# The linear term of three integration stages moved from TensorE to ScalarE and GpSimd, and one clamp from VectorE to GpSimd

## The chip, the cores and the metric

The kernel runs on one core of a Trainium2 chip. The metric is the device time of one execution in microseconds. A core has TensorE (PE, with weight loads listed apart as PEld), VectorE (DVE), ScalarE (ACT), GpSimd (POOL) and SyncE (SP), which issues the DMAs. Each engine works through its own queue in order, and semaphores tie the queues together.

## What is computed

Two layers, each a token mixer followed by a feed-forward block. The change lies in the mixer of the first layer, a coupled oscillator integrated over 32 time steps with the classical fourth-order Runge-Kutta rule. The state is q and p, of 128 batch rows by 256 features; x gives the drive of each step.

```python
def _derivative(q, p, drive, coupling, bias):
    i_couple = jnp.tanh(q) @ coupling.T
    dq = q - q ** 3 / 3.0 - p + drive + i_couple + bias
    dp = EPSILON * (q + ALPHA - BETA * p)
    return (dq, dp)

def _rk4_step(q, p, drive, coupling, bias):
    dq1, dp1 = _derivative(q, p, drive, coupling, bias)
    dq2, dp2 = _derivative(q + 0.5 * DT * dq1, p + 0.5 * DT * dp1, drive, coupling, bias)
    ...
    q_next = q + DT / 6.0 * (dq1 + 2 * dq2 + 2 * dq3 + dq4)
    p_next = p + DT / 6.0 * (dp1 + 2 * dp2 + 2 * dp3 + dp4)
    q_next = jnp.clip(q_next, -CLAMP, CLAMP)
    p_next = jnp.clip(p_next, -CLAMP, CLAMP)
    return (q_next, p_next)
```

Every q of the 32 steps then goes through a feed-forward block with block-quantized operands, and is added to x. The second layer (attention within a row's 32 tokens, then a feed-forward block with Hadamard rotations) follows on all 4096 tokens.

## The kernel before

The kernel has two phases. The first takes the 32 steps one after the other: `step` integrates q and p, and `ffn0` does the feed-forward block of that step's q and prepares the normalized, transposed input of the second layer (`xnT`). `ffn0` feeds nothing back into the recurrence, so it may run behind it, as far as its buffers reach. The second phase takes the 4096 tokens in 32 groups; its first item waits for the last `xnT`. Early in the first phase the weights of the first layer are quantized (POOL and DVE), from about step 24 on those of the second (ACT and DVE).

Nothing is issued in the order in which it is written. Every operation is an item with an engine, a cost in microseconds, the buffers that it reads and writes, and a rank. `Work.order` plans all items of both phases: a list scheduler, run forwards and backwards 40 times with priorities from the run before, that keeps the order with the earliest modelled end. Buffers take slots from pools (`slim`: 18 of 128x256 in SBUF; `ps_sum`: 3 of 128x256 in PSUM; `ps_stage`: 2 banks; `states`: 6), so a pool also limits how far work can run ahead. Where the plan leaves PE idle, small matmuls on zeros (L1354) are put in.

A step has four slopes. Slope i takes a state q_i (q, q2, q3, m4) and makes

- tanh of q_i on ACT (L594), and from it four 128x128 matmuls with the coupling matrix (L601, eight records each time since the data is fp32), which add to the PSUM tile `ps[i]`;
- a scaled square of q_i on ACT (L595), and from it the cube, square times q_i, on POOL (L608).

The next state is a `nest` (L552, one DVE operation: first operand times a constant, plus or minus the second) of `ps[i]` and the cube; after the fourth slope the new q is made by a saturating sum on DVE (L645). Into `ps[i]` go further an opening matmul on zeros (L497), a nest with p, x or w for the old state, and `plus` (L587): a matmul of a scaled identity with the drive or with a state. The eye matmuls `plus(1, 1, q2)`, `plus(2, 2, q3)` and `plus(3, 5, m4)` carry the linear term that belongs to the slope at q2, q3 and m4. `plus(3, 4, q3)` and the four with the drive are others. The slope at q has no such matmul: its linear term is in the constants K.

p is carried scaled and shifted. x, w and z are sums in PSUM that later stages need; z, which becomes the next p, is built in place over p by four nests, and is clamped in place on DVE (L653) at the end of the step. The next step's first nests read p and the new q.

Per step, `ffn0` adds on PE a transpose of q, eight bf16 512-column matmuls (L929), eight 256-column ones (L976) and a transpose; on DVE block maxima, scalings and clips; on POOL the multiplications by block scales (L914, L956, L964), the root (L993, L994) and, but for the last five steps, gain and shift (L1003, L1007).

Of the kernel before, what the change touches and what calls it, by code (L numbers as in the profile page):

```python
# [14 lines left out]
AF = mybir.ActivationFunctionType  # L15
ALU = mybir.AluOpType
# [4 lines left out]
P = 128  # L21
# [5 lines left out]
CLAMP = 20.0  # L27
# [12 lines left out]
PE, DVE, ACT, POOL, SP = "PE", "DVE", "ACT", "POOL", "SP"  # L40


def rk4():

    h, m = DT, DT * EPSILON  # L50

    def unit(i):
        return [float(i == n) for n in range(5)]

    def lin(*terms):
        return [sum(a * v[n] for a, v in terms) for n in range(5)]

    P1, q, Q2, Q3, Q4 = (unit(i) for i in range(5))
    s1 = lin((1.0, q), (-BETA, P1))
    P2 = lin((1.0, P1), (m / 2.0, s1))  # L60
    s2 = lin((1.0, Q2), (-BETA, P2))
    P3 = lin((1.0, P1), (m / 2.0, s2))
    s3 = lin((1.0, Q3), (-BETA, P3))
    P4 = lin((1.0, P1), (m, s3))
    s4 = lin((1.0, Q4), (-BETA, P4))
    end = lin((1.0, P1), (m / 6.0, s1), (m / 3.0, s2), (m / 3.0, s3), (m / 6.0, s4))
    last = lin((-1 / 3, q), (1 / 3, Q2), (2 / 3, Q3), (1 / 3, Q4), (-h / 6.0, P4))
    return P2, P3, end, last
# [31 lines left out]
class Work:  # L100
# [17 lines left out]
    def add(  # L118
        self, engine, cost, fn, reads=(), writes=(), fills=(), rank=0.0, table=None, port=False,
        tail=0.0, after=(), records=8, small=False, behind=(),  # L120
    ):
        item = Item(engine, cost, fn, rank, table, port, tail, records)
        item.small, item.behind = small, behind
        needs = list(after)
        for b in reads:
            needs += b.writers
        for b in writes:
            needs += b.writers + b.readers
        for b in reads:
            b.readers.append(item)  # L130
        for b in (*writes, *fills):
            b.writers.append(item)
        item.bufs = list(dict.fromkeys((*reads, *writes, *fills)))
        item.outs = (*writes, *fills)
        for b in item.bufs:
            b.left += 1
        item.after = list(dict.fromkeys(needs))
        self.items.append(item)
        return item
# [183 lines left out]
def kernel(  # L323
# [22 lines left out]
    nc = tc.nc  # L346
# [13 lines left out]
    def tile_of(name, shape, dtype=F32):  # L360
        return const.tile(shape, dtype, name=name)


    def slots(name, n, count, dtype=F32):
        return [Slot(tile_of(f"{name}{i}", [P, n], dtype)) for i in range(count)]
# [8 lines left out]
    slim = slots("slim", N, 18)  # L374
# [8 lines left out]
    def banks(name, n, count):  # L383

        tiles = [ps_1.tile([P, HALF], F32, name=f"{name}{i}") for i in range(-(-count * n // HALF))]
        return [
            Slot(t[:, k : k + n], f"{name}{i}") for i, t in enumerate(tiles) for k in range(0, HALF, n)
        ][:count]
# [3 lines left out]
    ps_sum = banks("ps_sum", N, 4)  # L392
# [29 lines left out]
    add = work.add  # L422
# [15 lines left out]
    def two(ap):  # L438
        return ap.rearrange("p (c k) -> p c k", c=NC)
# [38 lines left out]
    P2, P3, END, LAST = rk4()  # L478
    S = -END[4]
    h = DT  # L480
    K = (1.0 + h / 2, 1.0 - h / 2 * P2[1], 1.0 - h * P3[1])
    EYES = (h / 2 / K[0], h / 2 / K[1], h / K[2], h / 6, LAST[3], -LAST[4] - h / 6)
    C_SCALES = (*EYES[:3], -h / 6)
    CUBES = tuple((c / 3.0) ** 0.5 for c in (h / 2, h / 2, h, h / 6))
    eyes = []
    for i, c_eye in enumerate(EYES):
        eye = tile_of(f"eye{i}", [P, P])
# [6 lines left out]
    def opened(dst, rank, after=()):  # L494
        add(
            PE, 0.11,
            lambda: nc.tensor.matmul(dst.ap, lhsT=zeros[:, :P], rhs=zeros, start=True, stop=False),  # L497
            [], [dst], rank=rank, after=after,
        )
# [31 lines left out]
    for m in range(NC):  # L531
# [4 lines left out]
        sl = slice(m * P, (m + 1) * P)  # L536
        for i, (c_scale, b_c, c_mat) in enumerate(zip(C_SCALES, b_coup, coup)):
            add(
# [7 lines left out]
    stt = nc.vector.scalar_tensor_tensor  # L546
    MULT, ADD, SUB = ALU.mult, ALU.add, ALU.subtract

    def nest(dst, in0, scalar, in1, rank, op1=ADD):

        reads = [b for b in (in0, in1) if b is not dst]
        add(DVE, 0.335, lambda: stt(dst.ap, in0.ap, scalar, in1.ap, MULT, op1), reads, [dst], rank=rank)  # L552
# [26 lines left out]
    def step(t, q, p, d):  # L579
        rank = t - 500.0  # L580
        ps = [Buf(slots_) for slots_ in ps_stage]
        x, w, z = Buf(ps_sum), Buf(ps_sum), p
        q2, q3, m4, w2, qn = Buf(slim), Buf(slim), Buf(slim), Buf(slim), Buf(states)

        def plus(i, eye, src, cost=0.43):
            return add(
                PE, cost, lambda: nc.tensor.matmul(ps[i].ap, lhsT=eyes[eye], rhs=src.ap, start=False, stop=False),  # L587
                [src], [ps[i]], rank=rank,
            )

        def slope(i, qi):

            th, sq = Buf(slim), Buf(slim)
            add(ACT, 0.32, lambda: nc.scalar.activation(th.ap, qi.ap, AF.Tanh), [qi], [th], rank=rank, table="silu")  # L594
            add(ACT, 0.31, lambda: nc.scalar.activation(sq.ap, qi.ap, AF.Square, scale=CUBES[i]), [qi], [sq], rank=rank)  # L595

            def mm():
                for c in range(NC):
                    for m in range(NC):
                        sl = slice(m * P, (m + 1) * P)  # L600
                        nc.tensor.matmul(  # L601
                            ps[i].ap[:, sl], lhsT=coup[i][:, c, sl], rhs=two(th.ap)[:, c, :],
                            start=False, stop=(c == NC - 1 and m == NC - 1),
                        )

            add(PE, 0.9, mm, [th, b_coup[i]], [ps[i]], rank=rank)
            add(
                POOL, 0.685, lambda: nc.gpsimd.tensor_tensor(sq.ap, sq.ap, qi.ap, MULT),  # L608
                [qi], [sq], rank=rank, port=True,
            )  # L610
            return sq

        for i in range(2):
            opened(ps[i], rank)
            nest(ps[i], p, -h / 2 * (1.0, P2[0])[i] * S / K[i], q, rank)
            if not i:
                started.append(work.items[-1])
            plus(i, i, d)
        nest(x, p, -h * P3[0] * S / K[2], q, rank)
        cube = slope(0, q)  # L620
        nest(w, p, LAST[0] * S / LAST[1], q, rank)
        nest(z, p, END[0] * S / END[1], q, rank)
        nest(q2, ps[0], K[0], cube, rank, SUB)
        plus(1, 1, q2)
        cube = slope(1, q2)
        opened(ps[2], rank)
        nest(ps[2], q2, -h * P3[2] / K[2], x, rank)
        plus(2, 2, d)
        nest(w2, w, LAST[1] / LAST[2], q2, rank)
        nest(z, z, END[1] / END[2], q2, rank)  # L630
        nest(q3, ps[1], K[1], cube, rank, SUB)
        plus(2, 2, q3)
        cube = slope(2, q3)
        opened(ps[3], rank)
        add(ACT, 0.27, lambda: nc.scalar.mul(ps[3].ap, w2.ap, LAST[2]), [w2], [ps[3]], rank=rank)
        plus(3, 3, d)
        plus(3, 4, q3)
        nest(z, z, END[2] / END[3], q3, rank)
        nest(m4, ps[2], -K[2], cube, rank)
        plus(3, 5, m4)  # L640
        cube = slope(3, m4)
        nest(z, z, -END[3] / END[4], m4, rank)
        add(
            DVE, 0.335,
            lambda: nc.vector._custom_dve(  # L645
                TENSOR_ADD_SAT, out=qn.ap, in0=ps[3].ap, in1=cube.ap, s0=CLAMP, s1=-CLAMP
            ),
            [ps[3], cube], [qn], rank=rank,
        )
        edge = ALPHA / BETA  # L650
        add(
            DVE, 0.335,
            lambda: nc.vector.tensor_scalar(  # L653
                z.ap, z.ap, (-CLAMP - edge) / S, (CLAMP - edge) / S, ALU.min, ALU.max
            ),
            [], [z], rank=rank,
        )
        return qn, z


    def mx_scales(amax, nb, rank, mul, inv_slots):
# [360 lines left out]
    p = b_p  # L1022
# [9 lines left out]
    for t in range(T):  # L1032
        d = d_next
        if t + 1 < T:
            x_of[t + 1] = load_x(x_step, t + 1, t - 501.0)
            d_next = drive(t + 1, t - 499.9)
        q, p = step(t, q, p, d)
        ffn0(t, q)
# [378 lines left out]
```

## Time and profile before

| | us |
|---|---|
| median of 3 runs | 867.8 |
| lowest, highest | 867.76, 870.64 |
| the profiled execution | 868.0 |
| its span, first to last instruction | 866.2 |
| busy in the span: PE, PEld | 795.1, 598.6 |
| busy in the span: DVE, ACT, POOL | 732.2, 494.0, 615.9 |

A profile is of one execution, and what is added up from its rows stands against that execution's own time. Busy is the time covered by an engine's records; records of neighbouring instructions overlap, on PE most of all, so a covered engine need not be full. The granted PE clock was 0.986 over the span. In group lines the mean duration of one instruction stands after the busy time, and after the second bar the engine's idle time just ahead of these instructions, with what ended it. In timeline lines the first number is the start, the second how long the piece lasts, and the bracket holds the idle time before it and what ended it.

### The profile page before, as it was taken

The numbers are of one execution on the slowest core, as the hardware profiler recorded it, in microseconds if no ns is written. First come the engines' busy times: TensorE is split into PE (matmuls) and PEld (weight loads), VectorE is DVE, ScalarE is ACT, GpSimd is POOL, SyncE is SP. The second block draws the span as 40 slices with busy tenths as digits, with TensorE's granted clock in tenths as the row PEclk, the third lists the DMA queues.
The fourth block names the chain that finished last, engine by engine and source line by source line (L and its number), as shares of the span: only waits on it lengthen the run. The fifth ranks groups of instructions, "written<-read, shape, count | busy, mean of one in ns | idle before, by whom it ended". The sixth has DMA issues, their size and how long they took to land. (4 is left out here: it accounts for less than half of the span.)

```text
span 866.2 us, 26286 instructions
## 1 busy us (share of the span) xinstructions
PE 795.1 (92%) x10506; PEld 598.6 (69%) x10506; DVE 732.2 (85%) x1863; ACT 494.0 (57%) x1009; POOL 615.9 (71%) x955
## 2 busy tenths in 40 slices
PE   7789999999999999997789999999999999899986
PEld 4566778877788788775456667666667676576765
DVE  6889989999989999998677887778878788887694
ACT  3233465655466665754335667666767555776755
POOL 5698898888768888899574776656685676676320
PEclk9999999999999999999799999999999999999999
DMA  7222232313122242435500113221221221221334
GB/s 241 84 38 53 59 82 59 74 49 83 35 65 68 70 134 56 92 67 110 117 2 15 27 39 65 49 49 32 52 50 48 56 48 42 48 43 46 60 68 86
DMA packets 128891, 55.53 MB, mean 64 GB/s; under 512 B 102144, under 2 KB 127616, under 8 KB 128768
## 3 DMA queue, kind: packets, MB, share of 16 engines
q1 hardware_dynamic: 128768, 53.85, 26.9%
q8 instruction: 82, 1.34, 0.6%
q14 instruction: 41, 0.34, 0.1%
HBM read 21.32 MB, written 8.39 MB: 34 GB/s over the span
## 5 line engine op out<-in xcount | busy, mean ns | idle before, releaser
L1294 POOL TENSOR_TENSOR wide<-wide 128x512 f32<-128x512 f32 x116 | 149.1, 1306 | 68.7 <-DVE wide L1278 33.6
L601 PEld LDWEIGHTS ps_stage<-slim,coup 128*128 128x128 f32 x1024 | 129.3, 192 | 18.1 <-ACT slim L594 10.6
L601 PE MATMUL ps_stage<-slim,coup 128*128 128x128 f32 x1024 | 139.4, 279 | 0.6 <-ACT slim L594 0.3
L608 POOL TENSOR_TENSOR slim<-slim,slim 128x256 f32<-128x256 f32 x96 | 72.4, 755 | 27.7 <-ACT slim L595 23.0
L587 PE MATMUL ps_stage<-slim,eye 128*128 128x256 f32 x256 | 76.6, 392 | 8.1 <-DVE slim L552 7.8
L587 PE MATMUL ps_stage<-drives,eye 128*128 128x256 f32 x256 | 79.2, 392 | 3.3 <-DVE ps_stage L552 2.0
L956 POOL TENSOR_TENSOR mid<-mid,tiny 128x512 f32<-128x512 f32 x64 | 66.2, 1047 | 3.7 <-DVE tiny L678 3.2
L964 POOL TENSOR_TENSOR wide_bf<-mid,tiny 128x512 bf16<-128x512 fp8e4 x64 | 66.5, 1050 | 1.4 <-DVE mid L888 1.1
L594 ACT ACTIVATE slim<-slim 128x256 f32<-128x256 f32 x96 | 39.3, 409 | 47.4 <-DVE slim L552 44.6
L1305 PE MATMUL ps_two<-had_ffn,wide 128*128 128x128 f32 x512 | 63.3, 278 | 1.3 <-DVE wide L1278 1.2
L595 ACT ACTIVATE slim<-slim 128x256 f32<-128x256 f32 x96 | 39.2, 408 | 43.1 <-DVE slim L552 43.0
L1305 PEld LDWEIGHTS ps_two<-had_ffn,wide 128*128 128x128 f32 x512 | 59.9, 192 | 5.4 <-ACT wide L1300 1.9
L1125 PE MATMUL ps_one<-w_qkv_sb,xnT 128*128 128x512 f32 x128 | 60.7, 599 | 0.5 <-DVE mid L1196 0.2
L1313 ACT ACTIVATE wide<-ps_two,magic,tiny 128x1024 f32<-128x1024 f32 x32 | 38.5, 1203 | 39.5 <-DVE tiny L1079 28.0
L587 PEld LDWEIGHTS ps_stage<-slim,eye 128*128 128x128 f32 x256 | 42.0, 190 | 24.0 <-DVE slim L552 16.1
L1294 DVE TENSOR_TENSOR wide<-wide 128x512 f32<-128x512 f32 x76 | 53.3, 727 | 5.9 <-POOL wide L1294 5.9
L1278 DVE SCALAR_TENSOR_TENSOR wide<-ps_two,tiny,mid 128x512 f32<-128x512 f32 x64 | 46.4, 737 | 12.0 <-ACT mid L1271 11.3
L1207 PEld LDWEIGHTS ps_one<-v_pad,mid 32*32 32x32 f32 x4096 | 42.2, 106 | 20.8 <-issue 15.4
L1271 ACT ACTIVATE mid<-ps_two,tiny 128x512 f32<-128x512 f32 x64 | 43.0, 686 | 21.9 <-PE ps_two L1263 21.6
L1207 PE MATMUL ps_one<-v_pad,mid 32*32 32x17 f32 x4096 | 48.0, 181 | 4.5 <-issue 3.0
L587 PEld LDWEIGHTS ps_stage<-drives,eye 128*128 128x128 f32 x256 | 40.3, 193 | 12.3 <-DVE ps_stage L552 7.7
L1263 PEld LDWEIGHTS <-slim_bf 128*128 128x128 bf16 x256 | 24.0, 97 | 34.3 <-issue 8.3
(169 smaller groups left out, 2188.7 us busy)
## 6 DMA issues: line engine op xcount, KB each, us to landing
x_step<-in_x_dram SPq DMA_DIRECT2D x32, 128.0 KB, 2.1
x_add<-in_x_dram SPq DMA_DIRECT2D x32, 128.0 KB, 2.1
x_dram<-slim SPq DMA_DIRECT2D x32, 128.0 KB, 1.9
slim<-x_dram SPq DMA_DIRECT2D x32, 128.0 KB, 2.6
out_dram<-slim SPq DMA_DIRECT2D x32, 128.0 KB, 1.7
raws<-in_L_ffn_w_gate_dram SPq DMA_DIRECT2D x4, 512.0 KB, 4.8
raws<-in_L_ffn_w_up_dram SPq DMA_DIRECT2D x4, 512.0 KB, 6.3
raws<-in_L_ffn_w_down_dram SPq DMA_DIRECT2D x4, 512.0 KB, 4.0
```

What stands on the lines that cost most here:

```text
L587: PE, cost, lambda: nc.tensor.matmul(ps[i].ap, lhsT=eyes[eye], rhs=src.ap, start=False, stop=False),
L594: add(ACT, 0.32, lambda: nc.scalar.activation(th.ap, qi.ap, AF.Tanh), [qi], [th], rank=rank, table="silu")
L601: nc.tensor.matmul(ps[i].ap[:, sl], lhsT=coup[i][:, c, sl], rhs=two(th.ap)[:, c, :], start=False, stop=(c == NC - 1 and m == NC - 1),)
L608: POOL, 0.685, lambda: nc.gpsimd.tensor_tensor(sq.ap, sq.ap, qi.ap, MULT),
L956: lambda it=it, ks=ks: nc.gpsimd.tensor_tensor(blocks(it.ap), blocks(it.ap), spread(binv.ap[:, ks], BLOCK), MULT),
L964: lambda b8=b8, ks=ks, sl=sl: nc.gpsimd.tensor_tensor(blocks(bq.ap[:, sl]), blocks(b8.ap), spread(bscl.ap[:, ks], BLOCK), MULT),
L1125: nc.tensor.matmul(pqk.ap, lhsT=xnT_flat[:, c, tok], rhs=w_qkv_sb[:, c, : 2 * N], start=(c == 0), stop=(c == NC - 1),)
L1207: nc.tensor.matmul(by_v(po.ap)[row, hd, :], lhsT=by_head(exT.ap)[row, hd, :], rhs=v_pad.ap[row, hd, :], start=True, stop=True,)
L1271: lambda pgu=pgu, act=act: nc.scalar.activation(act.ap, pgu.ap[:, :HALF], AF.Silu, scale=sgu.ap[:, 0:1]),
L1278: lambda pgu=pgu, act=act, sl=sl: stt(it.ap[:, sl], pgu.ap[:, HALF:], sgu.ap[:, 1:2], act.ap, MULT, MULT),
L1294: eng.tensor_tensor(dv[:, :, e, :], sv[:, :, 0, :], sv[:, :, 1, :], op)
L1305: nc.tensor.matmul(pfh.ap[:, sl], lhsT=iT.ap[:, sl], rhs=had_ffn, start=True, stop=True)
```

## The change

In slopes 1 to 3 the linear term is no longer added to PSUM by an eye matmul. The square gets a constant added by an ACT Identity activation with a bias tile, in place, and POOL multiplies the result by q_i as before, which makes cube and linear term in one product. (CUBE names the engine for each slope; all four are POOL, so the DVE branch is never taken.) Slope 0 has no constant and is as before. The sixth eye is not made; a tile of four constants is.

z no longer lies over p: it has a PSUM slot of its own, its last nest writes to a `slim` tile, and POOL clamps that into another `slim` tile, the new p.

```diff
-    EYES = (h / 2 / K[0], h / 2 / K[1], h / K[2], h / 6, LAST[3], -LAST[4] - h / 6)
+    EYES = (h / 2 / K[0], h / 2 / K[1], h / K[2], h / 6, LAST[3])
+    LINEAR = (0.0, -h / 2, -h, -LAST[4] - h / 6)
+    CUBE = (POOL, POOL, POOL, POOL)
     C_SCALES = (*EYES[:3], -h / 6)
+    linear = tile_of("linear", [P, 4])
+    for i, c_linear in enumerate(LINEAR):
+        nc.gpsimd.memset(linear[:, i : i + 1], c_linear)
...
-        x, w, z = Buf(ps_sum), Buf(ps_sum), p
+        x, w, z = Buf(ps_sum), Buf(ps_sum), Buf(ps_sum)
...
             add(PE, 0.9, mm, [th, b_coup[i]], [ps[i]], rank=rank)
+
+            if CUBE[i] == DVE:
+                add(DVE, 0.335, lambda: stt(sq.ap, sq.ap, LINEAR[i], qi.ap, ADD, MULT), [qi], [sq], rank=rank, port=True)
+                return sq
+            if LINEAR[i]:
+                add(
+                    ACT, 0.31,
+                    lambda: nc.scalar.activation(sq.ap, sq.ap, AF.Identity, bias=linear[:, i : i + 1]),
+                    [], [sq], rank=rank,
+                )
             add(
                 POOL, 0.685, lambda: nc.gpsimd.tensor_tensor(sq.ap, sq.ap, qi.ap, MULT),
                 [qi], [sq], rank=rank, port=True,
...
-        plus(1, 1, q2)
         cube = slope(1, q2)
...
-        plus(2, 2, q3)
         cube = slope(2, q3)
...
         nest(m4, ps[2], -K[2], cube, rank)
-        plus(3, 5, m4)
         cube = slope(3, m4)
-        nest(z, z, -END[3] / END[4], m4, rank)
...
         edge = ALPHA / BETA
+        z_in = Buf(slim)
+        nest(z_in, z, -END[3] / END[4], m4, rank)
+        pn = Buf(slim)
         add(
-            DVE, 0.335,
-            lambda: nc.vector.tensor_scalar(
-                z.ap, z.ap, (-CLAMP - edge) / S, (CLAMP - edge) / S, ALU.min, ALU.max
+            POOL, 0.45,
+            lambda: nc.gpsimd.tensor_scalar(
+                pn.ap, z_in.ap, (-CLAMP - edge) / S, (CLAMP - edge) / S, ALU.min, ALU.max
             ),
-            [], [z], rank=rank,
+            [z_in], [pn], rank=rank, port=True,
         )
-        return qn, z
+        return qn, pn
```

## The prediction

> **What bounds the kernel now.** I read the page's slices first, then the busy time by stage, then single stages of the recurrence in the timeline, then who waits.
>
> ```profile
> PE   7789999999999999997789999999999999899986
> DVE  6889989999989999998677887778878788887694
> ACT  3233465655466665754335667666767555776755
> POOL 5698898888768888899574776656685676676320
> ```
>
> The 32 integration steps end near slice 18 (of 21.7 us each). Up to there PE, DVE and POOL are all nearly full and ACT is half empty. What lies after, about 436 us, is not touched by the change, though the planner orders both phases anew.
>
> ```profile
> 31.00:97.00 66.00, 58.00 (x351) 42.81 (x350) 62.40 (x141) 23.29 (x62) 55.22 (x42) 1.00 0.21 41
> 97.00:323.00 226.00, 223.15 (x1486) 178.49 (x1485) 210.37 (x606) 131.17 (x376) 189.93 (x257) 1.00 0.30 72
> 323.00:398.00 75.00, 72.74 (x484) 57.48 (x483) 72.77 (x206) 44.35 (x125) 68.35 (x91) 1.00 0.32 72
> 398.00:430.00 32.00, 21.93 (x120) 14.45 (x120) 25.81 (x56) 14.43 (x37) 24.15 (x31) 0.79 0.57 126
> ```
>
> The columns are the window, its length, busy PE, PEld, DVE, ACT, POOL, then PE's clock, the DMA share and GB/s. The windows are cut at the ends of steps: L645 starts at 97.2 (step 5), 322.9 (step 25) and 398.0 (step 31). So a step takes 225.7/20 = 11.3 us in the middle, 12.5 late, 11.3 to 15.8 early. In the middle PE is covered for 223 of 226 us, DVE for 210; late DVE is at 97%.
>
> Covered time overstates, as records overlap. I took the spacing of back-to-back pairs from the timeline instead: a coupling matmul 0.112, an eye matmul pair 0.43, a bf16 512-column one 0.215, a 256-column one or a transpose 0.109; DVE 0.331 for 256 columns and 0.595 for 512; POOL 0.685, 1.005, 0.573, 0.515 and 0.273 for its lines; ACT 0.307 for 256 columns. Times the counts per step: PE 32x0.112 + 8x0.43 + 8x0.215 + 8x0.109 + 5x0.109 + 6x0.109 = 10.8 us; DVE 18x0.331 + 6x0.595 + six tiny ones of 0.08 = 10.0; POOL 4x0.685 + 4x1.005 + 0.573 + 2x0.685 + 0.79 = 9.5; ACT about 5.7. Of 11.3 us PE is 96% used, DVE 88%, POOL 84%.
>
> One pass of the recurrence (nest, tanh and square, coupling matmuls beside the cube, next nest):
>
> ```profile
> 216.90 0.41 DVE L552 SCALAR_TENSOR_TENSOR slim<-ps_stage,slim 128x256 f32<-128x256 f32 x1
> ...
> 217.34 0.42 ACT L594 ACTIVATE slim<-slim 128x256 f32<-128x256 f32 x1 [1.16 <-DVE slim L552]
> ...
> 217.41 0.65 PE L587 MATMUL ps_stage<-slim,eye 128*128 128x256 f32 x2
> 217.66 0.40 ACT L595 ACTIVATE slim<-slim 128x256 f32<-128x256 f32 x1
> ...
> 218.00 1.06 PE L601 MATMUL ps_stage<-slim,coup 128*128 128x128 f32 x8
> ...
> 218.14 0.72 POOL L608 TENSOR_TENSOR slim<-slim,slim 128x256 f32<-128x256 f32 x1 [0.91 <-ACT slim L595]
> ...
> 219.17 0.42 DVE L552 SCALAR_TENSOR_TENSOR slim<-ps_stage,slim 128x256 f32<-128x256 f32 x1 [0.52 <-PE ps_stage L601]
> ```
>
> The cube is done at 218.86, the matmuls at 219.06, and the nest waits for the matmuls. A pass takes 2.27 us here; four average 11.3 (3.17, 2.83, 2.61, 2.74), so about 2.2 us a step is waiting for engines that do other work. Over steps 6 to 23 I compared both ends in each stage: the cube ends last in 22, 22 and 44% of stages 1, 2 and 3, and lies on average 0.66, 0.49 and 0.48 us ahead of the nest that reads it.
>
> ```profile
> L552 DVE SCALAR_TENSOR_TENSOR slim<-ps_stage,slim 128x256 f32<-128x256 f32 x60 | 25.0, 417 | 4.9 <-PE ps_stage L601 4.3 <-POOL slim L608 0.4 <-POOL tiny L993 0.2
> L645 DVE CUSTOM_DVE_ANT_0 states<-ps_stage,slim 128x256 f32<-128x256 f32 x21 | 8.8, 419 | 5.5 <-POOL slim L608 2.2 <-PE ps_stage L601 1.4 <-PE ps_po L497 1.1
> ```
>
> In the middle DVE idles 4.3 us for PE before these nests and 0.4 for the cube. The xnT copy of a step (L1017) comes 82 to 104 us after the end of that step from step 7 to 26, seven to nine steps late: the feed-forward work is backed up. So the middle is a matter of capacity, PE first, with DVE close behind.
>
> **What the Trainium skill says.** "Perfetto Trace Analysis", Identifying the Most-Contended Engine, warns that matmul busy time is no measure of headroom and that the weight-load share is to be used: PEld is 79% in the middle, so PE is less full than its row says; my spacing sum agrees in kind (96, not 99%). "ScalarE: Activation LUTs", Rules for kernel authors, prices an activation with a [128,1] bias at about 0.3 us plus 0.83 ns an element, 0.51 us at 256; this trace has 510 ns for such an op below. Its section on table sets says that identity is in every set; L572 runs it here between tanh and square with no table load. "GPSIMD Engine Reference", Engine selection, calls one-input ops roughly line-rate, two-input ones about twice DVE's time: the trace has 727 ns for L608 on POOL against about 415 for a DVE op of that size.
>
> **The change part by part.** The profiled execution took 868.0 us (span 866.2, 1.8 around it); the runs' median, 867.8, is the same within 0.2, so sums against 868.0 need no shift.
>
> *Three eye matmuls go* (1,1,q2; 2,2,q3; 3,5,m4): 3x0.43 = 1.29 us of PE a step, 25.8 in the middle, 41 in all. PE falls to 9.5 a step.
>
> *Three Identity activations come*, between square and cube.
>
> ```profile
> L1250 ACT ACTIVATE slim_bf<-slim,neg_magic 128x256 bf16<-128x256 f32 x32 | 16.3, 510 | 0.5
> ```
>
> The same function with a bias tile takes 510 ns; it adds about 0.4 of engine time (L1313 and L1317, dependent and back to back, leave 0.02 between), so ACT goes from 5.7 to 6.9 of 11.3, still the emptiest. But it puts 0.53 us (0.02 + 0.51) ahead of the cube. With the cubes' starts left where POOL was busy until then, only 0.21 us a step passes the nest's start in the middle, 4.6 us in 32 steps; with every POOL wait kept behind the new op, 16.7. Queued behind Identity on ACT: the tanh, if the planner puts the square first, and so the coupling matmuls. The planner prices Identity at 0.31 against 0.4, so its order is a little early there.
>
> *The clamp of p goes from DVE to POOL*: DVE loses 0.33 a step, 10.6 in all (10.0 to 9.7); the last nest of z stays and writes SBUF, at the same price. The trace has no one-input POOL op of 256 columns:
>
> ```profile
> L842 POOL TENSOR_SCALAR had_ffn<-had_ffn x1: 297/297/297, 13.1 to 13.1; 128x128 f32<-128x128 f32 x1
> L993 POOL TENSOR_SCALAR tiny<-tiny x32: 190/190/1110, 103.8 to 427.0; 128x1 f32<-128x1 f32 x32
> ```
>
> From 190 at one column and 297 at 128, 0.40; four of L837 take 1.40, 0.35 each, which gives 0.46. I take 0.45; it can't exceed the two-input 0.73 nor undercut 0.30. POOL: 9.5 to 9.9, 14 us in all. p's reader also needs the new q, and the clamp is ready a whole pass earlier (m4's square, cube and the final sum follow it), so it is hidden unless it sits in front of the fourth cube: then 0.45 on the path.
>
> *Buffers*: z gets its own PSUM slot of three; only in step 0, where the first p holds one, must it wait for x's release, for nothing urgent. Two more slim buffers a step of 18, short-lived: nothing, at worst a delayed ffn0 item. Set-up: four tiny memsets for one eye, about nothing.
>
> *Sum.* The fullest engine in the middle was PE at 10.8; it becomes POOL at 9.9, with DVE 9.7 and PE 9.5. At the same 96% that is 10.3 us a step, -1.0, or -20 over 20 steps; but three engines at one level and a cube without slack won't be packed as one was, and the 0.2 us of late cubes comes off. I take -0.45 a step: -9. Early and late DVE is the fuller one (95, 97%): -0.33 for 12 steps is -4, which POOL's +0.45 (91% late) mostly takes back: -1. Total -10: 858.
>
> **The rivals.**
> *The cube becomes the path.* Stages 1 to 3 end on square, Identity, POOL: POOL at 88% makes the cube wait (it waits 0.24 to 0.47 there now, within its slack), and PE's freed time is left idle. It decides once the cube ends last in well over half of those stages. Price: 4.6 to 16.7 us by the working above, and up to 0.45 for each clamp in front of a cube; I take +11: 879. For it: ACT-POOL-DVE hops, and the 44% in stage 3 already. Against it: 4.3 us of waits for PE against 0.4 for the cube.
> *It moves nothing.* DVE is covered 93 to 97%; if its tiny dependent ops can't be packed tighter, and POOL takes back what DVE gives, 866 to 868. Against it: DVE loses work too.
>
> **Numbers.** Under 0.5% (4.3 us) can't be told from no change here. PE's relief 0.50, at 858 (own range 846 to 863); the cube on the path 0.36, 879 (872 to 890); nothing 0.14. The new order of the second phase adds some us either way, an estimate from nothing but its length. Range: the full relief, -20 and -4, would give 844; I take 846, and 884 for most of the slower case.
>
> **What would show it.** Right: PE's weight loads in the middle fall from 79% to about 72%; steps at 10.8 to 10.9; Identity near 510 ns; POOL above 86%; the cube last in about half the stages 1 to 3. Wrong: steps at 11.5 or more with PE idle before the coupling matmuls or DVE idle for POOL L608's line; a clamp in front of a cube; the xnT lag shrunk to two or three steps (the recurrence is then the limit, not capacity).

## The result, and the profile after

The changed kernel takes 931.2 us (930.43 to 933.34) against 868.4 in runs beside it: a ratio of 1.072, interval 1.069 to 1.075. The forecast was 858, with a range from 846 to 884. The profiled execution took 930.43 us with a span of 927.9, 61.7 more than before.

The page's slices of the changed kernel (23.2 us each):

```profile
PE   7777788888898898788868889999989998999986
DVE  5888998899899999999967778978869877798794
ACT  3333465655566575665533465665557677655764
POOL 5767787777879988988856549745666657488330
```

PE has less to do, as was meant: many an eight stands where nines stood. A part of that only comes of longer steps, since a kernel of the next section that keeps every eye matmul (clamp_only) shows PE covered for 206 us of the middle instead of 223. The recurrence and its tail now reach to slice 21. The same stretches of time as before, in which the slower kernel gets through fewer steps (length, busy PE, PEld, DVE, ACT, POOL, clock, DMA share, GB/s):

```profile
31.00:97.00 66.00, 52.34 (x281) 38.32 (x281) 55.41 (x107) 23.83 (x62) 46.22 (x37) 0.84 0.15 32
97.00:323.00 226.00, 193.09 (x1211) 140.96 (x1210) 208.19 (x512) 130.96 (x373) 184.15 (x242) 0.99 0.24 57
323.00:398.00 75.00, 62.67 (x403) 45.39 (x402) 71.25 (x175) 47.60 (x132) 64.88 (x85) 1.00 0.37 92
```

In the 226 us of the middle DVE is busy as long as before (208 against 210) while it issues 512 instructions instead of 606. So DVE got slower, not idler. Which instructions it is, the groups of the same window say (count, then busy us and mean ns of one, then idle before and what ended it). First three groups of the kernel before:

```profile
L552 DVE SCALAR_TENSOR_TENSOR ps_sum<-ps_sum,states 128x256 f32<-128x256 f32 x60 | 25.0, 422 | 0.1
L552 DVE SCALAR_TENSOR_TENSOR ps_stage<-ps_sum,states 128x256 f32<-128x256 f32 x40 | 16.7, 426 | 1.1 <-PE ps_stage L497 0.3
...
L608 POOL TENSOR_TENSOR slim<-slim,states 128x256 f32<-128x256 f32 x20 | 14.6, 728 | 4.5 <-DVE ps_sum L552 3.1 <-ACT slim L595 1.4
```

Then the changed kernel:

```profile
L557 DVE SCALAR_TENSOR_TENSOR ps_sum<-slim,states 128x256 f32<-128x256 f32 x53 | 37.7, 714 | 0.3
L623 POOL TENSOR_TENSOR slim<-slim,slim 128x256 f32<-128x256 f32 x51 | 37.2, 730 | 20.7 <-ACT slim L619 17.5 <-DVE ps_sum L557 2.9
L557 DVE SCALAR_TENSOR_TENSOR ps_stage<-slim,states 128x256 f32<-128x256 f32 x36 | 26.0, 738 | 0.7 <-DVE ps_sum L680 0.4
L619 ACT ACTIVATE slim<-slim,linear 128x256 f32<-128x256 f32 x51 | 25.2, 493 | 0.0
...
L557 DVE SCALAR_TENSOR_TENSOR slim<-ps_stage,slim 128x256 f32<-128x256 f32 x51 | 21.3, 417 | 5.5 <-POOL slim L623 3.4 <-PE ps_stage L606 1.8
L600 ACT ACTIVATE slim<-slim 128x256 f32<-128x256 f32 x51 | 21.2, 416 | 72.0 <-DVE slim L557 71.8
...
L623 POOL TENSOR_TENSOR slim<-slim,states 128x256 f32<-128x256 f32 x18 | 16.0, 892 | 1.8 <-DVE ps_sum L557 1.3 <-ACT slim L600 0.5
...
L667 POOL TENSOR_SCALAR slim<-slim 128x256 f32<-128x256 f32 x17 | 6.8, 401 | 3.6 <-DVE tiny L692 2.2 <-DVE slim L557 1.4
```

The L557 lines are all one helper's nests, on tiles of one size. Those with an operand in PSUM take 417 ns. Those written `<-slim,states`, which read the new p and q, take 714 and 738: both their operands now lie in SBUF. They were `<-ps_sum,states` before, at 422 and 426 ns. The POOL cube that shares its time with them (`<-slim,states`) grew as well, from 728 to 892. And the added ACT activation and the POOL clamp cost about what was estimated: 493 and 401 ns.

DVE and POOL just after the end of a step, from the timeline (start, length of the piece, instruction), first before and then in the changed kernel:

```profile
201.74 0.75 DVE L552 SCALAR_TENSOR_TENSOR ps_sum<-ps_sum,states 128x256 f32<-128x256 f32 x2
201.80 0.73 POOL L608 TENSOR_TENSOR slim<-slim,states 128x256 f32<-128x256 f32 x1 [0.73 <-ACT slim L595]
```

```profile
203.45 1.29 DVE L557 SCALAR_TENSOR_TENSOR ps_stage<-slim,states 128x256 f32<-128x256 f32 x2
203.70 0.75 POOL L623 TENSOR_TENSOR slim<-slim,states 128x256 f32<-128x256 f32 x1 [0.49 <-ACT slim L600]
...
204.42 0.91 POOL L1017 TENSOR_TENSOR slim<-slim,gain 128x256 f32<-128x256 f32 x1
204.66 0.95 DVE L557 SCALAR_TENSOR_TENSOR ps_sum<-slim,states 128x256 f32<-128x256 f32 x1
205.40 0.79 POOL L1021 TENSOR_TENSOR slim<-slim,shift 128x256 f32<-128x256 f32 x1
```

Two nests that fitted into 0.75 us beside a cube on POOL now take 1.29, and the next one 0.95, each time beside a POOL operation that reads two SBUF tiles. Over the whole trace the 155 such nests last 424 ns where no POOL operation overlaps them (24 of them), 848 on average where it is mostly a slope-0 cube, and 887 where it is mostly L970, a 512-column product on POOL. Their sum is 119.6 us, against 65.6 for the nests that read p before: 54.0 more.

The first phase, up to the first matmul with w_qkv, ends at 484.4 us instead of 431.3: 53.1 more. The second takes 443.4 instead of 434.9.

My account before the experiments, the **port theory**: DVE and POOL contend for SBUF when a DVE operation has both operands there; by moving p out of PSUM the change put five nests of each step into that contention. The Trainium skill states it outright ("SBUF — State Buffer", Who interferes with whom): a DVE instruction with two SBUF inputs contends with a GpSimd instruction that reads SBUF, while one with at most one such input does not. The nests at 417 and near 900 ns agree. Its rivals were the **cube theory** (the Identity in front of the cube lengthens the recurrence) and the **clamp theory** (POOL's extra work and the hand-over cost it). One more comes in below: that z no longer lies over p but needs a PSUM slot of its own.

### The profile page after: what moved, and what is told of

It is laid out like the page before. It is cut to its first block, busy times and chain, and to the rows that moved or that the text cites. A ratio compares the mean times of both kernels' runs of the same rounds, so it can differ in the third digit from the quotient of the medians.

```text
span 927.9 us, 26239 instructions
## 1 busy us (share of the span) xinstructions
PE 798.9 (86%) x10425; PEld 582.4 (63%) x10425; DVE 783.1 (84%) x1831; ACT 525.4 (57%) x1101; POOL 641.1 (69%) x990
## 4 chain that ended last, share of the span: by engine, by line
DVE 38%; POOL 21%; PE 18%; ACT 10%; issue 9%; DMA 4%; SPq 0%; POOLq 0%; DVEq 0%; ACTq 0%
DVE ps_sum L557 6%; POOL wide L1308 5%; DVE ps_stage L557 5%; DVE wide L1308 4%; POOL slim L623 3%; DVE slim L557 3%; PE ps_stage L606 3%; DVE tiny L1085 2%; DVE tiny L702 2%; DVE wide L1292 2%; POOL wide_bf L978 2%; PE ps_one L1139 2%; PE ps_two L1277 2%; DVE mid L902 2%; ACT wide L1327 1%
## 5 line engine op out<-in xcount | busy, mean ns | idle before, releaser
L606 PE MATMUL ps_stage<-slim,coup 128*128 128x128 f32 x1024 | 146.5, 287 | 10.0 <-ACT slim L599 8.3
L600 ACT ACTIVATE slim<-slim 128x256 f32<-128x256 f32 x96 | 39.9, 416 | 143.6 <-DVE slim L557 143.3
L592 PE MATMUL ps_stage<-drives,eye 128*128 128x256 f32 x256 | 85.1, 416 | 18.9 <-DVE ps_stage L557 17.5
L978 POOL TENSOR_TENSOR wide_bf<-mid,tiny 128x512 bf16<-128x512 fp8e4 x64 | 69.1, 1085 | 9.8 <-DVE mid L902 9.1
L970 POOL TENSOR_TENSOR mid<-mid,tiny 128x512 f32<-128x512 f32 x64 | 70.8, 1113 | 5.1 <-DVE tiny L692 4.9
L557 DVE SCALAR_TENSOR_TENSOR ps_sum<-slim,states 128x256 f32<-128x256 f32 x93 | 68.7, 746 | 0.4
L502 PE MATMUL ps_stage<-zeros 128*128 128x256 bf16 x128 | 35.0, 275 | 37.8 <-DVE slim L557 30.5
L1308 DVE TENSOR_TENSOR wide<-wide 128x512 f32<-128x512 f32 x76 | 63.0, 865 | 2.9 <-POOL wide L1308 2.7
L1285 ACT ACTIVATE mid<-ps_two,tiny 128x512 f32<-128x512 f32 x64 | 42.7, 686 | 23.2 <-PE ps_two L1277 22.9
L557 DVE SCALAR_TENSOR_TENSOR ps_stage<-slim,states 128x256 f32<-128x256 f32 x62 | 49.1, 810 | 1.0 <-DVE ps_sum L680 0.4
L619 ACT ACTIVATE slim<-slim,linear 128x256 f32<-128x256 f32 x96 | 47.4, 493 | 0.1
```

Source lines behind the costliest of these rows:

```text
L606: nc.tensor.matmul(ps[i].ap[:, sl], lhsT=coup[i][:, c, sl], rhs=two(th.ap)[:, c, :], start=False, stop=(c == NC - 1 and m == NC - 1),)
L970: lambda it=it, ks=ks: nc.gpsimd.tensor_tensor(blocks(it.ap), blocks(it.ap), spread(binv.ap[:, ks], BLOCK), MULT),
L978: lambda b8=b8, ks=ks, sl=sl: nc.gpsimd.tensor_tensor(blocks(bq.ap[:, sl]), blocks(b8.ap), spread(bscl.ap[:, ks], BLOCK), MULT),
L1308: eng.tensor_tensor(dv[:, :, e, :], sv[:, :, 0, :], sv[:, :, 1, :], op)
```

## The experiments

Times are medians, ratios go with the kernel before on the same chip. "Nests" gives the sum of the nests that read p, minus 65.6 us, and the two last columns how much longer each phase is than in the profile before. These three are of one profiled execution, which lies up to 4.3 us from the median.

| | us | ratio (95%) | nests | first phase | second phase |
|---|---|---|---|---|---|
| the changed kernel | 931.2 | 1.072 (1.069 to 1.075) | +54.0 | +53.1 | +8.5 |
| clamp_only | 924.6 | 1.063 (1.060 to 1.065) | +55.7 | +54.8 | +1.2 |
| p_in_sbuf | 926.4 | 1.065 (1.062 to 1.068) | +46.4 | +48.3 | +9.4 |
| linear_only | 891.6 | 1.025 (1.022 to 1.028) | +0.1 | +8.3 | +14.3 |
| p_copied_back | 882.5 | 1.015 (1.011 to 1.018) | 0.0 | +17.2 | +1.6 |
| after_pinned | 923.9 | 1.063 (1.058 to 1.067) | +54.1 | +53.0 | -1.9 |
| linear_pinned | 879.9 | 1.011 (1.008 to 1.015) | +0.3 | +8.9 | +2.4 |
| nests_on_port | 930.6 | 1.072 (1.067 to 1.077) | +27.6 | +58.4 | +0.9 |
| two_in_sbuf | 897.9 | 1.033 (1.028 to 1.038) | +24.2 | +25.3 | +4.7 |
| three_in_sbuf | 910.8 | 1.049 (1.046 to 1.052) | +24.5 | +29.8 | +10.6 |
| linear_slope1_pinned | 871.0 | 1.003 (1.002 to 1.004) | 0.0 | +0.8 | +2.0 |
| clamp_copied_pinned | 870.0 | 1.001 (1.000 to 1.003) | +0.1 | +0.3 | -0.3 |

**The two halves of the change.** First the kernel before with the new treatment of p alone:

```diff
-        x, w, z = Buf(ps_sum), Buf(ps_sum), p
+        x, w, z = Buf(ps_sum), Buf(ps_sum), Buf(ps_sum)
...
-        nest(z, z, -END[3] / END[4], m4, rank)
...
+        z_in = Buf(slim)
+        nest(z_in, z, -END[3] / END[4], m4, rank)
+        pn = Buf(slim)
...
-        return qn, z
+        return qn, pn
```

> The kernel before with the change's treatment of p alone: z in its own PSUM slot, the clamp on POOL, the new p in SBUF; the linear terms stay on PE. Port theory (the five nests of a step that read p together with q now have both operands in SBUF and are stretched while POOL works): 915 to 932 us, these nests at 740 to 800 ns. Cube theory (the Identity in front of the cube lengthens the recurrence): 866 to 872, as no Identity is there. Clamp theory (POOL's extra work and the hand-over to it cost the time): 915 to 932 as well.

Measured 924.6: with no Identity and all eye matmuls kept, nearly the whole loss is there. The cube theory can't hold it.

Then the changed kernel with p as it was:

```diff
-        x, w, z = Buf(ps_sum), Buf(ps_sum), Buf(ps_sum)
+        x, w, z = Buf(ps_sum), Buf(ps_sum), p
...
+        nest(z, z, -END[3] / END[4], m4, rank)
...
-        return qn, pn
+        return qn, z
```

> The changed kernel with p as before (z built over p in PSUM, clamp in place on DVE); the linear terms are taken with the cube. Port theory: 856 to 872 us, the nests that read p at 420 ns. Cube theory: 905 to 932, steps at 12.5 us or more. Clamp theory: 856 to 872.

Measured 891.6, between the theories' bands: not the big loss, but no gain either. The linear half costs something by itself; see below.

**Where p lies, without POOL's clamp.** The kernel before, but DVE's clamp writes to SBUF, and z, which can't lie over a p in SBUF, has its own PSUM slot:

```diff
-        x, w, z = Buf(ps_sum), Buf(ps_sum), p
+        x, w, z = Buf(ps_sum), Buf(ps_sum), Buf(ps_sum)
...
+        pn = Buf(slim)
         add(
             DVE, 0.335,
             lambda: nc.vector.tensor_scalar(
-                z.ap, z.ap, (-CLAMP - edge) / S, (CLAMP - edge) / S, ALU.min, ALU.max
+                pn.ap, z.ap, (-CLAMP - edge) / S, (CLAMP - edge) / S, ALU.min, ALU.max
             ),
-            [], [z], rank=rank,
+            [z], [pn], rank=rank,
         )
-        return qn, z
+        return qn, pn
```

> The kernel before, but the DVE clamp writes the new p to an SBUF tile instead of in place in PSUM; no work for POOL, no Identity. Port theory: 905 to 928 us, the five nests at 720 to 800 ns. Cube theory and clamp theory: 865 to 871, nests at 420 ns.

Measured 926.4. The groups of its nests that read p:

```profile
L552 DVE SCALAR_TENSOR_TENSOR ps_sum<-slim,states 128x256 f32<-128x256 f32 x93 | 63.5, 687 | 0.3
L552 DVE SCALAR_TENSOR_TENSOR ps_stage<-slim,states 128x256 f32<-128x256 f32 x62 | 47.0, 776 | 0.3
```

The clamp stays on its engine and only its destination moves, with z's slot behind it, and that costs 56 us: 48 in the first phase, the rest in the second, whose order is a new one (see below). POOL got no work, so the clamp theory falls too. That it isn't z's slot is shown by two_in_sbuf and three_in_sbuf below, where z stays over p and the nests that read p from SBUF are about as slow.

**Back into PSUM.** The changed kernel with z over p again, and an ACT copy of the POOL-clamped p into a PSUM slot:

```diff
-        x, w, z = Buf(ps_sum), Buf(ps_sum), Buf(ps_sum)
+        x, w, z = Buf(ps_sum), Buf(ps_sum), p
...
+        p_next = Buf(ps_sum)
+        add(ACT, 0.31, lambda: nc.scalar.copy(p_next.ap, pn.ap), [pn], [p_next], rank=rank)
-        return qn, pn
+        return qn, p_next
```

> The changed kernel, clamp on POOL and linear terms with the cube, but ACT copies the clamped p to a PSUM slot and the nests read it there. Port theory: 858 to 880 us, nests at 420 ns. Cube theory and clamp theory: 915 to 940.

Measured 882.5, 2.5 above the port theory's band and far from the others'. The nests are back:

```profile
L557 DVE SCALAR_TENSOR_TENSOR ps_sum<-ps_sum,states 128x256 f32<-128x256 f32 x93 | 38.2, 423 | 0.3
...
L557 DVE SCALAR_TENSOR_TENSOR ps_stage<-ps_sum,states 128x256 f32<-128x256 f32 x62 | 24.4, 424 | 1.8 <-ACT ps_sum L673 1.0
```

An added instruction per step, 382 ns on ACT, wins back 49 of 63 us, 7 of them by the profiles in the second phase. And with the linear terms left on PE (the same clamp and copy in the kernel before, the second phase in a fixed order as explained next):

> The linear terms on PE as before, the clamp on POOL, its result copied to PSUM by ACT, second phase in the order of the kernel before. If POOL's clamp itself costs next to nothing: 866 to 873 us. If its 0.45 us of POOL and the two hand-overs get in the way of the cubes: 876 to 886.

Measured 870.0, ratio 1.001: a clamp on POOL, with the copy behind it, costs nothing that can be told, once nothing reads its result together with another SBUF tile on DVE.

**The second phase.** It isn't touched, yet its length differs by up to 14 us between these kernels. I wrote the planner's result for the kernel before (order of the second phase's items, buffer slots, filler matmuls) into the changed kernel:

```diff
     issue = work.order()
+    second_items = [i for i in work.items if i.rank >= PHASE_TWO]
...
+    issue = [i for i in issue if i.rank < PHASE_TWO] + [second_items[k] for k in PIN_ORDER]
```

> The changed kernel with the second phase in the order, the buffer slots and the filler matmuls that the planner gave the kernel before; the first phase is planned as in the changed kernel. Order theory (the second phase is 8.5 us longer only because the planner orders it anew): 919 to 926 us, second phase 434 to 437. Spill theory (something of the first phase, the PE clock or late loads, slows the second): 929 to 934, second phase 442 to 445.

Measured 923.9, with a second phase of 433.0 us, a little under the order theory's band for it and far from the other's: order theory. The same for the linear half alone:

> The linear terms with the cube alone, p as before in PSUM, second phase in the order of the kernel before. Order theory: 875 to 880 us, 12 to 17 less than without the pinned order. Spill theory: 888 to 894. What is left over 868 to 871 is the cost of the linear part in the first phase: cube theory 6 to 11 us.

Measured 879.9 with a second phase of 437.3. So 7 us of the changed kernel's loss and 12 of linear_only's come from a new plan of untouched work. In part it may be the same contention: of the Hadamard butterflies of the second phase (sums and differences of pairs of columns) 116 run on POOL and 76 on DVE, the latter with both operands in SBUF. The DVE ones before, in the changed kernel, and with the pinned order:

```profile
L1294 DVE TENSOR_TENSOR wide<-wide 128x512 f32<-128x512 f32 x76 | 53.3, 727 | 5.9 <-POOL wide L1294 5.9
```

```profile
L1308 DVE TENSOR_TENSOR wide<-wide 128x512 f32<-128x512 f32 x76 | 63.0, 865 | 2.9 <-POOL wide L1308 2.7
```

```profile
L1460 DVE TENSOR_TENSOR wide<-wide 128x512 f32<-128x512 f32 x76 | 53.8, 734 | 6.0 <-POOL wide L1460 6.0
```

**Was it only a bad plan?** The planner of this kernel lets no two items marked `port` overlap in its plan, on whichever engine they run. The nests weren't marked, as p was in PSUM. I marked the five:

```diff
-    def nest(dst, in0, scalar, in1, rank, op1=ADD):
+    def nest(dst, in0, scalar, in1, rank, op1=ADD, port=False):
...
-        nest(x, p, -h * P3[0] * S / K[2], q, rank)
+        nest(x, p, -h * P3[0] * S / K[2], q, rank, port=True)
...
```

> The changed kernel, but the planner is told that the nests reading p share the port with POOL, so that it plans them and POOL's work apart. Planning theory (the loss is mostly a plan that puts them together): 880 to 905 us, nests at 420 to 550 ns. Capacity theory (POOL is busy for three quarters of the first phase, so the nests can't be kept apart without stalling one or the other): 912 to 932.

Measured 930.6: capacity theory. The collisions became rarer, but the time did not fall:

```profile
L557 DVE SCALAR_TENSOR_TENSOR ps_sum<-slim,states 128x256 f32<-128x256 f32 x93 | 55.3, 603 | 0.3
...
L557 DVE SCALAR_TENSOR_TENSOR ps_stage<-slim,states 128x256 f32<-128x256 f32 x62 | 36.0, 599 | 0.5 <-PE ps_stage L502 0.2
```

The nests lost half of their excess, and the first phase is still 58.4 us longer. In steps 6 to 23 the coupling matmuls of slope 0, which queue behind the nest into their bank, now start 1.8 us after the end of the tanh instead of 0.86 in the changed kernel: a planned wait took the place of the stall.

**Which of the five count.** The kernel before, plus an ACT copy of p to SBUF that some of the nests read:

```diff
+        z.twin = Buf(slim)
+        add(ACT, 0.31, lambda t2=z.twin: nc.scalar.copy(t2.ap, z.ap), [z], [z.twin], rank=rank)
...
-            nest(ps[i], p, -h / 2 * (1.0, P2[0])[i] * S / K[i], q, rank)
+            nest(ps[i], p2, -h / 2 * (1.0, P2[0])[i] * S / K[i], q, rank)
```

(p2 is the twin of the last step's p.) The two into the stage banks:

> The kernel before, with an ACT copy of the clamped p to SBUF; the two nests into the stage banks, which the recurrence waits for, read the copy, the three for x, w and z read PSUM. Capacity theory (each stretched nest costs DVE time, wherever it stands): two fifths of the 56 us of all five, 888 to 896 us. Path theory (only what delays the next state counts): 898 to 915.

The other three, with the first two on PSUM:

> The counterpart of two_in_sbuf: the nests for x, w and z read the SBUF copy of p, the two into the stage banks read PSUM. Capacity theory: three fifths of 56 us, 898 to 908. Path theory: 872 to 886, since x, w and z are wanted later than the stage banks.

Measured 897.9 and 910.8. The first lies between its two bands, the second just above the capacity band; the path theory's 872 to 886 for it is excluded. Their second phases, with a new order each, hold 4.7 and 10.6 us of that. Their first phases grew by 25.3 and 29.8 us, their nests by 24.2 and 24.5. So it matters little whether a stretched nest is one that the recurrence waits for: DVE takes its instructions in order, and x, w and z stand between the new q and the nest for q2. That is where the time shows: over steps 6 to 23 it is 3.16 us from the new q to q2 before, and 4.30 in the changed kernel. In the kernels whose nests read p from SBUF the first phase grows by about what these nests grow (within 5.3 us), but for nests_on_port. What the added ACT copy costs by itself wasn't measured.

**The linear half.** linear_pinned is the plain price of taking the linear terms with the cube: 1.1%, about 11 us. PE was relieved as meant: its 192 records of the three eye matmuls are gone, though about 100 small matmuls on zeros were put into the gaps, and its middle window shows 155 us of weight loads against 178 before:

```profile
97.00:323.00 226.00, 210.76 (x1358) 155.44 (x1358) 213.45 (x601) 148.50 (x422) 189.33 (x255) 1.00 0.30 71
```

But the recurrence got slower. My comparison of both ends of each slope over steps 6 to 23, before and in linear_pinned, counted from the start of the instruction that makes a state:

| slope | us from state to state | cube ends last | tanh starts after the state |
|---|---|---|---|
| 0 | 3.16, 3.02 | 11%, 17% | 0.70, 0.62 |
| 1 | 2.82, 2.97 | 22%, 50% | 0.69, 0.74 |
| 2 | 2.61, 2.90 | 22%, 56% | 0.63, 0.80 |
| 3 | 2.74, 3.01 | 44%, 67% | 0.62, 0.80 |

Slopes 1 to 3 lose 0.15, 0.29 and 0.27 us; slope 0, which has no Identity, gains 0.14. The planner puts the square first to give the longer cube path a start (in 51 of the 54 stages 1 to 3, before in 23), which holds up the tanh and the matmuls, and still the cube ends last in 31 of the 54, before in 16.

How much of this the kernel feels is less plain. The 20 middle steps take 240.7 us instead of 225.7, 15 more, but the whole first phase only 8.9 more, for the feed-forward work fell less far behind and left a shorter tail: 27.8 us after the last step instead of 33.3. And DVE is no emptier for the slower recurrence; it idles 14.6 us in those steps, before 15.6. One such slope alone, where the cube had most room:

```diff
-    EYES = (h / 2 / K[0], h / 2 / K[1], h / K[2], h / 6, LAST[3])
-    LINEAR = (0.0, -h / 2, -h, -LAST[4] - h / 6)
+    EYES = (h / 2 / K[0], h / 2 / K[1], h / K[2], h / 6, LAST[3], -LAST[4] - h / 6)
+    LINEAR = (0.0, -h / 2, 0.0, 0.0)
...
+        plus(2, 2, q3)
         cube = slope(2, q3)
...
+        plus(3, 5, m4)
         cube = slope(3, m4)
```

> As linear_pinned, but only the slope at q2 takes its linear term with the cube; the other two keep their eye matmuls. Cube theory (each such slope costs the recurrence 0.15 to 0.3 us a step, and PE's relief buys nothing): 871 to 876 us. Relief theory (one third of PE's relief where the cube had most room, at little cost on the path): 860 to 868.

Measured 871.0, ratio 1.003: at the foot of the cube theory's band, and no gain. The relief theory is out, but the cube theory's reason isn't there either: slope 1 takes 2.85 us against 2.82, a step 11.31 against 11.32 (steps 6 to 23), and the cube ends last in 6 of 18 against 4. A third of PE's relief bought nothing even where the path hardly grew. None of these kernels is faster than the one before.

## Why the prediction was wrong

**The step that failed** is one line: "the last nest of z stays and writes SBUF, at the same price", with the line on buffers that calls two more slim tiles "nothing". I priced the instruction that writes p and not the five that read it. They went from one SBUF operand to two, and their mean from 423 to 772 ns: 54.0 us in 155 nests, where the sum had 0. p_in_sbuf shows it with POOL and PE left as they were, two_in_sbuf and three_in_sbuf with z's slot left as well; in p_copied_back and clamp_copied_pinned it is gone.

**The sum for the middle** failed too, in its -9: I read a PE that was 96% used as the bound. linear_pinned has the relief, PE is emptier, and the middle steps went from 11.3 to 12.0 us. DVE, which was to be the next to bind, doesn't explain it alone either: clamp_copied_pinned takes 11.4 us off DVE's busy time in the first phase and keeps PE's work, and its first phase is 0.3 us longer; p_copied_back relieves both and is slower than before. What fits all three is that the recurrence, with its waits from engine to engine, sets the pace together with what it queues behind; this is argued, not shown. The prediction's own sign for it, feed-forward work only two or three steps late, did not come: in linear_pinned it is 68 to 93 us late in steps 6 to 23, which is six to eight steps, so that lag doesn't tell the two apart.

**The slower rival**, the cube on the path, is what the linear half does: its mark was a cube that ends last in well over half of the stages, and it came out at 50, 56 and 67%, 57% together, which is over half but not well over; its 4.6 to 16.7 us hold the 11 measured. As an account of the whole change it failed, since that costs 63: in clamp_only, with no Identity, it costs 54 all the same.

**Right**: Identity (510 forecast, 493), the clamp (0.45, 0.401), its being hidden (clamp_copied_pinned), PE's weight loads only in part (72% forecast for the middle; 69% in linear_pinned and 62% in the changed kernel, where longer steps lower the share too). Mis-sized: "some us either way" for the new plan of the second phase was 7 and 12, one way.

The two halves don't add up: after_pinned, with both, is no slower than clamp_only (1.063 both). Why is open. A longer cube path doesn't simply find room behind the held-up nests: slopes 1 to 3 together take 8.62 us in after_pinned, 7.97 in clamp_only and 8.88 in linear_pinned, but slope 0, where the five nests are, takes 4.30 in after_pinned and 4.65 in clamp_only. p_copied_back lost 17 us in the first phase of its profile, where the linear terms alone lost 9 and the copied clamp alone nothing. That profile is of its slowest execution, 4.3 us over the median, and 11 of the 17 are lost by the end of step 5; over all executions its ratio, 1.015, can't be told from linear_pinned's 1.011.

## What to carry to other kernels

When a tile moves between PSUM and SBUF, list its readers and count the SBUF operands that each then has on DVE; beside a busy POOL a second one cost 0.35 us per 256-column operation here, and three quarters of the loss came back by copying the tile to PSUM on ACT, the least busy engine. An engine that is nearly full isn't yet the bound: taking work off PE here, or off DVE, bought nothing. Look at what a serial chain waits for, and think twice before lengthening its branches to empty an engine. Where a planner orders everything, pin the untouched part before a difference of 1% is explained.

## What had not been expected of the hardware

The stall is a wait for the other's end, not a slower pace. In the changed kernel 26 of the nests with both operands in SBUF overlap exactly one POOL operation of 256 columns or more. In 14 of them POOL had begun first and had 0.3 us or more still to run: the nest then ended 288 to 295 ns after POOL's operation did, whether that left it at 611 ns or, beside a 1024-column operation, at 2136. In 10 the nest had begun first, or within 10 ns: it took its usual 420 to 434 ns, and POOL's operation ended 463 to 908 ns after it. The last two met the final 0.06 us of a POOL operation and took 417 and 418. clamp_only (20 such nests behind POOL, 288 to 294 ns) and p_in_sbuf (21, 287 to 294 ns) show the same. So in these traces whichever begins first goes through, and the other ends as if most of its work began only when the first was done. A long POOL operation, not only a frequent one, is what makes a short DVE operation dear, and the slope-0 cubes on POOL pay likewise when a nest is ahead of them.

One kind of POOL operation held nothing up. The nests that overlapped mostly with L1008 (a power on 128x1, 0.55 us long, two SBUF inputs) lasted 423 ns, 18 of them, the same as with POOL idle; eight of these overlapped nothing else and began while it had 185 to 488 ns to run. So not every POOL record stands for a hold as long as itself; the skill's rule quoted above makes no such exception, and here the measurement decides. Whether it is the single column or the sort of operation, no run here tells apart.
